# The second layer's norm of a two-layer transformer: its factors by Newton's steps on VectorE, spread to all partitions through DRAM and applied to x where it lies, instead of on token rows that are turned back

## The chip, the cores and the metric

The kernel runs on one core of a Trainium2 chip. The metric is the device time of one execution in microseconds, the median of several runs. A core has TensorE (PE in the profile, with its weight loads as PEld), VectorE (DVE), ScalarE (ACT), GpSimd (POOL) and SyncE (SP), which here only issues DMA transfers. The on-chip memory (SBUF) has 128 partitions; TensorE writes its results to a second, small memory, PSUM, in banks of 128 x 512 numbers. The first number of a shape is always the partitions.

## What is computed

Two layers on x of 2 batches x 2048 tokens x 256 features, all in float32. Each layer normalizes x over the features, runs attention and a gated side branch on the result, and adds their product to x. The first layer has full attention and a recurrent mixture of experts, the second has attention in a window of 64 tokens to either side and a mixture of eight low-rank experts.

```python
def _layernorm(x, axis=-1, eps=1e-05):
    m = jnp.mean(x, axis=axis, keepdims=True)
    v = jnp.var(x, axis=axis, keepdims=True)
    return (x - m) / jnp.sqrt(v + eps)
...
    x = L0_attn_x
    xn = _layernorm(x, axis=-1)
    s = _L0_attn_ref(xn, ...)
    g = _silu(_L0_ffn_ref(xn, ...))
    x = x + s * g
    xn = _layernorm(x, axis=-1)
    s = _L1_attn_ref(xn, ...)
    g = _silu(_L1_ffn_ref(xn, ...))
    x = x + s * g
    return x
```

The change concerns the second `_layernorm` only.

## The kernel before

**Layout.** x, its normalized form xn and the gates gt lie in SBUF for the whole kernel, one tile per batch, with features on partitions: [128, 2, 2048], the 256 features being two halves of 128. A block is 512 tokens; a batch has four. The mean and the variance of a token run over features, that is over partitions[...]. So the norm goes through token rows.

**The second norm before.** `norm_there` (L114 to L126) takes half a block, 256 tokens: TensorE turns x by four transposes of 128 x 128 into a PSUM bank with tokens on partitions, one copy (L120) puts that into xn, where it rests, and VectorE takes `bn_stats` (L123) and `bn_aggr` (L125), which give mean and variance per token. `factors` (L98 to L102) makes from them, for all 16 tiles of a batch or for eight at once, 1/sqrt(var + eps) by a ScalarE square root (L100) and a VectorE reciprocal (L101), and -mean times that (L102). A factor is then one number per partition, so `norm_apply` scales a row tile with one instruction (L131 on ScalarE, L133 on VectorE). `norm_back` (L135 to L143) turns the block back on TensorE, eight transposes (L139) into two banks, and copies them into xn (L143).

**Attention of the first layer.** It has 32 items (batch, group of four heads, block of 512 queries). An item takes 16 steps of 128 keys. In a step TensorE makes scores for a maximum of an item six steps ahead (`sq`, L671), scores of this item (`sk`, L671), and the product of the last step's exponentials with v (`acc`, L747). `sk`, `acc` and everything small share one ring of four PSUM banks. ScalarE takes the exponential; the products are summed up in `av`: by a ScalarE copy and a GpSimd add (L760, L761) as a rule, but in the last 22 steps by one VectorE add (L755) that reads the bank. An item that is complete is divided by its denominators through small DMA transfers on SP (`ad`, `dn`, `rd`, then `recb`, the reciprocals spread over the heads' partitions), the last of them a GpSimd multiply (`divide`, L801). The very last item takes a shorter way by TensorE transposes (`last_there` L809 to L813, `last_back` L825). `project` (L833) is the output projection; its result times the gate (`upd`, L838, VectorE, one buffer) is added to x by GpSimd (L840).

**The order of the work.** The program is written step by step, and `at(s, f)` hangs a function behind step s. Within an engine the instructions run in the order in which they are written, which a scheduler may shift where `pin` does not hold them. In the last 22 steps, which no longer have `sq` work, batch 0's `norm_there` calls hang two steps apart, eight of them. After the last step a written list does the rest of batch 0: apply, back, the last item's projection, and the router's `gates` (L966, copy L970) and `tokens` (L974, copy L976) of the second layer for every block, then `normalized` (a softmax over eight experts).

**The stage between the layers.** Batch 1 is normalized here. Its calls alternate by hand with the second layer's key and query projections of batch 0 (`keys_queries`, L469, 16 jobs, twelve of them placed among the norm's calls), which give TensorE work while the other engines do theirs. Transposes use a ring of two banks (tag `l`), projections one of four (tag `o`), gates and tokens one more. Then come the experts (L1021 to L1037) and the second attention, which the change does not touch.

Of the kernel before, what the change touches and what calls it, by code (L numbers as in the profile page):

```python
# [10 lines left out]
F32 = mybir.dt.float32  # L11
I32 = mybir.dt.int32
AF = mybir.ActivationFunctionType
ALU = mybir.AluOpType
# [3 lines left out]
P = 128  # L18
D = 256
NC = D // P  # L20
H = 16
HD = D // H
NG = 4
HP = 32
HV = HD + 1
DEN = HD - 1
TB = 512
# [11 lines left out]
def two_layers(ctx: ExitStack, tc: tile.TileContext, a, out):  # L39
# [58 lines left out]
    def factors(f, mv, issue=lambda i: i):  # L98

        issue(nc.scalar.activation(f[:, 0, :], mv[:, :, 1], AF.Sqrt, bias=eps_t))  # L100
        nc.vector.reciprocal(f[:, 0, :], f[:, 0, :])  # L101
        nc.vector.scalar_tensor_tensor(f[:, 1, :], mv[:, :, 0], -1.0, f[:, 0, :], ALU.mult, ALU.mult)  # L102


    def resting(b, n, half):
        return xn[b][:, half, bass.ts(n, TB)].rearrange("p (t d) -> p t d", d=D)

    def norm_there(b, n, half, bank, tmp, mv, copy, issue=lambda i: i):

        H2 = QT // 2  # L110
        xt = bank().rearrange("p (t d) -> p t d", d=D)
        for t in range(H2):
            for c in range(NC):
                i = nc.tensor.transpose(  # L114
                    xt[:, t, bass.ts(c, P)], x[b][:, c, bass.ds(n * TB + (half * H2 + t) * P, P)], ident
                )
                if t + c == 0:
                    issue(i)
        rest = resting(b, n, half)
        copy(rest, xt)  # L120
        st = tmp.tile([P, H2, 6], F32, name="st2", tag="st2", bufs=1)
        for t in range(H2):
            nc.vector.bn_stats(st[:, t, :], rest[:, t, :])  # L123
        for t in range(H2):
            nc.vector.bn_aggr(mv[:, half * H2 + t, :], st[:, t, :])  # L125

    def norm_apply(b, n, f):
        for t in range(QT):
            rest = resting(b, n, t // 2)[:, t % 2, :]
            if t % 2:  # L130
                nc.scalar.activation(rest, rest, AF.Identity, scale=f[:, 0, t : t + 1], bias=f[:, 1, t : t + 1])  # L131
            else:
                nc.vector.tensor_scalar(rest, rest, f[:, 0, t : t + 1], f[:, 1, t : t + 1], ALU.mult, ALU.add)  # L133

    def norm_back(b, n, bank):  # L135
        xb = [bank() for _ in range(NC)]
        for c in range(NC):
            for t in range(QT):
                nc.tensor.transpose(  # L139
                    xb[c][:, bass.ts(t, P)], resting(b, n, t // 2)[:, t % 2, bass.ts(c, P)], ident  # L140
                )
        for c in range(NC):
            (nc.scalar.copy, nc.vector.tensor_copy)[c](xn[b][:, c, bass.ts(n, TB)], xb[c])  # L143

    def layer_norms(blocks, tmp, ps, between=lambda r: None):

# [329 lines left out]
    def attention(A, scale, local, final, start=None, projected=False):  # L476
# [19 lines left out]
        with ExitStack() as st:  # L496
# [357 lines left out]
            def at(s, f, *args):  # L854
                after.setdefault(s, []).append((f, args))
# [26 lines left out]
                at(0, start)  # L882
            if not local:
                single = lambda: pm.tile([P, TB], F32, name="xb", tag="m")
                mv = op.tile([P, NT, 2], F32, name="mv", tag="mv")
                nf = op.tile([P, 2, NT], F32, name="nf", tag="nf")
                tile_of = lambda n: slice(n * QT, (n + 1) * QT)
                logit = {}

                def back(n):  # L890
                    norm_back(0, n, single)
                    logit[n] = ep.tile([P, TB], F32, name="sl", tag="e")[:, :P]
# [6 lines left out]
                for f, *args in (  # L899
                    (last_there, last),  # L900
                    (norm_apply, 0, 0, nf[:, :, tile_of(0)]),
                    (last_back, last),
                    (back, 0),
                    (norm_apply, 0, 1, nf[:, :, tile_of(1)]),
                    (project, last, 0),
                    (back, 1),
                    (project, last, 1),
                    (norm_apply, 0, 2, nf[:, :, tile_of(2)]),
                    (lambda: gates(single()[:, :P], logit[0], 0, 0),),
                    (norm_apply, 0, 3, nf[:, :, tile_of(3)]),  # L910
                    (back, 2),
                    (lambda: tokens(single()[:, :P], logit[0], 0, 0),),
                    (lambda: gates(single()[:, :P], logit[1], 0, 1),),
                    (back, 3),
                    (lambda: tokens(single()[:, :P], logit[1], 0, 1),),
                    (lambda: gates(single()[:, :P], logit[2], 0, 2),),
                    (lambda: gates(single()[:, :P], logit[3], 0, 3),),
                    (lambda: tokens(single()[:, :P], logit[2], 0, 2),),
                    (lambda: tokens(single()[:, :P], logit[3], 0, 3),),
                    (normalized, op, 0),  # L920
                ):
                    at(total, f, *args)
            fetch(0)
# [71 lines left out]
    with tc.tile_pool(name="gw", bufs=1) as gw, tc.tile_pool(name="tb", bufs=2) as tb, tc.tile_pool(  # L995
# [49 lines left out]
        with tc.tile_pool(name="pl", bufs=1, space=PSUM) as pl:  # L1045
            bank = lambda: pl.tile([P, TB], F32, name="xb", tag="l", bufs=2)
            small = lambda: pl.tile([P, TB], F32, name="s", tag="s")[:, :P]
            mv = gw.tile([P, NT, 2], F32, name="mv1")
            nf = gw.tile([P, 2, NT], F32, name="nf1")
            tile_of = lambda n: slice(n * QT, (n + 1) * QT)  # L1050
            two = lambda r: slice(2 * r * QT, 2 * (r + 1) * QT)
            sl = {}

            def there(n):
                for half in range(2):
                    norm_there(1, n, half, bank, tb, mv[:, tile_of(n), :], nc.scalar.copy)
# [22 lines left out]
            norm_apply(1, 0, nf[:, :, tile_of(0)])  # L1079
            norm_apply(1, 1, nf[:, :, tile_of(1)])  # L1080
            there(2)
            project(1)
            there(3)
            factors(nf[:, :, two(1)], mv[:, two(1), :])
            project(1)
            norm_back(1, 0, bank)
            project(1)
            logits(0)
            norm_back(1, 1, bank)
            project(1)  # L1090
            tokens(small(), sl[0], 1, 0)
            logits(1)
            norm_apply(1, 2, nf[:, :, tile_of(2)])
            norm_apply(1, 3, nf[:, :, tile_of(3)])
            project(2)
            tokens(small(), sl[1], 1, 1)
            norm_back(1, 2, bank)
            project(1)
            logits(2)
            norm_back(1, 3, bank)  # L1100
# [12 lines left out]
            for n in range(NB):  # L1113
                experts(1, n)()
# [72 lines left out]
```

## Time and profile before

| | us |
|---|---|
| median of 3 runs | 2532.57 (2530.11 to 2535.89) |
| the profiled execution, its own time | 2535.19 |
| its span in the profile | 2533.5 |
| last steps of the first attention (last 22 of 512) | to 2108 |
| rest of batch 0's norm and its router | 2108 to 2124 |
| batch 1's norm beside projections | from 2124 |

| group | line | count | mean ns |
|---|---|---|---|
| exponentials, ScalarE 128 x 512 | L687 | 2048 | 602 |
| scores, TensorE 32 x 512 | L671 | 5632 | 533 |
| weighted values, TensorE 128 x 512 | L747 | 4096 | 605 |
| sum of products, GpSimd 128 x 512 | L761 | 459 | 1265 |

The mean granted TensorE clock is 0.999 of full speed. Engine names in the profile are those given above; a line such as "L747" is a line of the kernel as printed. In a group, "out<-in" names the tiles written and read. In a timeline the first number is the start in us from the span's begin, the second how long the instruction or the row of like instructions ran, and the bracket behind it how long the engine had been idle before and which instruction of another engine it was waiting for.

### The profile page before, as it was taken

What the parts mean: (1) busy time and instruction counts of PE and PEld (TensorE: products, weight loads), DVE (VectorE), ACT (ScalarE), POOL (GpSimd) and SP (SyncE); (2) the same over time, 40 slices, a digit from 0 to 9 for tenths busy, and PEclk for the clock granted to TensorE, in tenths of its full rate; (3) what the DMA queues carried; (4) which work ended last, traced back from release to release, by engine and by line L of the source; (5) the groups of instructions that cost most, each with busy time, mean ns of one, the idle gap of its engine ahead of it and who ended that gap; (6) DMA issues with size and microseconds to landing.
All of it is one profiled execution on the core that took longest, in us unless ns stands there. A gap on an engine that the chain in (4) does not pass through costs nothing.

```text
span 2533.5 us, 47883 instructions
## 1 busy us (share of the span) xinstructions
PE 2511.0 (99%) x18896; PEld 1058.6 (42%) x18896; DVE 1697.5 (67%) x2741; ACT 1628.0 (64%) x3204; POOL 878.0 (35%) x827
## 2 busy tenths in 40 slices
PE   8999999999999999999999999999999999999999
PEld 6444444444333333333333333333333334457766
DVE  4143333258888888888777788888888765238986
ACT  5400000126888888888888888888888886237755
POOL 0000000201444444444444444444444420016887
PEclk9999999999999999999999999999999999999999
DMA  4031111220000000000000000000000002121221
GB/s 159 3 84 51 52 51 39 88 79 14 6 10 23 8 8 23 8 8 23 8 8 23 6 8 25 6 10 24 6 10 6 6 10 68 43 100 60 87 98 63
DMA packets 59733, 89.67 MB, mean 35 GB/s; under 512 B 21064, under 2 KB 25544, under 8 KB 58228
## 3 DMA queue, kind: packets, MB, share of 16 engines
q1 hardware_dynamic: 57636, 85.31, 10.3%
q8 instruction: 148, 2.42, 0.4%
q10 hardware_dynamic: 1872, 1.31, 0.2%
q14 instruction: 77, 0.63, 0.1%
HBM read 55.99 MB, written 22.59 MB: 31 GB/s over the span
## 4 chain that ended last, share of the span: by engine, by line
PE 80%; DVE 0%; ACT 0%; DMA 0%; issue 0%; POOL 0%; ACTq 0%; DVEq 0%
PE sk L671 25%; PE acc L747 23%; PE sq L671 20%; PE pp L469 5%; PE pr L833 2%; PE pp L529 2%; PE po L1025 1%; PE pt L1021 1%; PE po L1033 1%; PE xb L114 0%; PE xb L139 0%; PE pmx L723 0%; PE of L825 0%; PE pw L1008 0%; DMA recb<-rd 0%
## 5 line engine op out<-in xcount | busy, mean ns | idle before, releaser
L683 DVE TENSOR_REDUCE part<-sq 128x2 f32<-128x1024 f32 x1024 | 1207.0, 1221 | 287.6 <-PE sq L671 287.4
L687 ACT ACTIVATE e<-sk 128x512 f32<-128x512 f32 x2048 | 1057.5, 602 | 215.8 <-PE sq L671 204.6
L671 PE MATMUL sk<-q,k 32*128 32x512 f32 (+2 forms) x5632 | 1135.1, 533 | 1.2 <-ACT xn L687 0.9
L671 PE MATMUL sq<-k,q 31*128 31x512 f32 (+2 forms) x5120 | 1129.1, 569 | 0.5 <-DVE part L683 0.5
L761 POOL TENSOR_TENSOR av<-av,more 128x512 f32<-128x512 f32 x459 | 580.7, 1265 | 931.9 <-ACT more L760 925.2
L671 PEld LDWEIGHTS sk<-q,k 32*128 32x128 f32 x5632 | 521.4, 184 | 603.2 <-ACT e L687 519.0
L747 PE MATMUL acc<-e,v 128*32 128x512 f32 x4096 | 546.7, 605 | 0.0
L671 PEld LDWEIGHTS sq<-k,q 31*128 31x128 f32 x5120 | 403.1, 183 | 22.9 <-DVE part L683 12.6
L760 ACT COPY more<-acc 128x512 f32<-128x512 f32 x459 | 269.1, 586 | 0.0
L747 PEld LDWEIGHTS acc<-e,v 128*32 128x32 f32 x4096 | 81.8, 108 | 388.1 <-ACT e L687 379.0
L453 ACT ACTIVATE gt<-po 128x512 f32<-128x512 f32 x16 | 8.8, 594 | 321.1 <-PE po L449 321.1
L678 DVE CUSTOM_DVE_ANT_0 seen<-sq,mask 128x256 f32<-128x256 f32 (+1 forms) x512 | 175.7, 408 | 57.8 <-PE sq L671 54.3
L459 POOL TENSOR_TENSOR x<-x,up 128x512 f32<-128x512 f32 x16 | 25.1, 1589 | 450.1 <-DVE up L456 450.1
L440 DVE TENSOR_TENSOR xs<-we,px 128x512 f32<-128x512 f32 x64 | 44.0, 687 | 136.4 <-PE px L432 131.8
L692 POOL TENSOR_SCALAR_AFFINE_SELECT xn<-xn 128x512 f32<-128x512 f32 x172 | 106.2, 652 | 78.4 <-ACT xn L687 75.5
L432 PE MATMUL px<-xn,FV 128*128 128x512 f32 x256 | 121.2, 595 | 0.0
L436 PE MATMUL py<-cum,FW 128*128 128x512 f32 x256 | 120.5, 593 | 0.6 <-DVE cum L404 0.6
L416 PE MATMUL po<-pr,UO 128*128 128x512 f32 x256 | 119.0, 592 | 0.0
L687 ACT ACTIVATE xn<-sk 128x512 f32<-128x512 f32 x172 | 90.0, 600 | 41.6 <-PE sq L671 18.1
L442 DVE TENSOR_TENSOR pr<-xs,py 128x512 f32<-128x512 f32 x64 | 44.0, 688 | 64.4 <-PE py L436 64.2
L416 PEld LDWEIGHTS po<-pr,UO 128*128 128x128 f32 x256 | 48.6, 190 | 61.2 <-issue 61.2
L436 PEld LDWEIGHTS py<-cum,FW 128*128 128x128 f32 x256 | 48.4, 190 | 61.5 <-issue 59.8
(197 smaller groups left out, 1621.9 us busy)
## 6 DMA issues: line engine op xcount, KB each, us to landing
we<-wd SPq DMA_DIRECT2D x128, 128.0 KB
qd<-sb SPq DMA_DIRECT2D x48, 256.0 KB
xn<-av SPq DMA_DIRECT2D x59, 128.0 KB
recb<-rd SPq DMA_DIRECT2D x59, 128.0 KB
k<-qd SPq DMA_DIRECT2D x10, 512.0 KB
q<-qd SPq DMA_DIRECT2D x10, 512.0 KB
x<-in_x SPq DMA_DIRECT2D x8, 512.0 KB
qd<-elast SPq DMA_DIRECT2D x16, 256.0 KB
```

What stands on the lines that cost most here:

```text
L416: nc.tensor.matmul(po[oc], UO[:, ch, bass.ts(oc, P)], pr, start=(ch == 0), stop=False)
L432: nc.tensor.matmul(px, FV[:, c, bass.ts(ch, P)], xn[b][:, c, cols], start=(c == 0), stop=(c == NC - 1))
L436: nc.tensor.matmul(py, FW[:, c, bass.ts(ch, P)], cum[:, c, :], start=(c == 0), stop=(c == NC - 1))
L469: nc.tensor.matmul(ps, w[:, c, bass.ts(hf, P)], xn[b][:, c, bass.ts(n, TB)], start=(c == 0), stop=(c == NC - 1))
L671: nc.tensor.matmul(o, lhs, rhs, start=True, stop=True)
L678: nc.vector.tensor_tensor_reduce(seen[:, lo:hi], sq[:, d, t * 2 * P + lo : t * 2 * P + hi], mask[:, lo:hi], 1.0, LOWEST, ALU.add, ALU.max, ...
L683: nc.vector.tensor_reduce(pt[:, pair[0] : pair[1] + 1, t, kb], sq, AX.X, ALU.max)
L687: nc.scalar.activation(e, t, AF.Exp, scale=scale)
L692: nc.gpsimd.affine_select(out=e[:, :, c, :], in_=e[:, :, c, :], compare_op=ALU.is_ge, fill=0.0, base=0, pattern=[[0, 4], [sign, P]], chann ...
L747: nc.tensor.matmul(acc[hp[j], o : o + hi - lo], vs[b][:, kt, vcols(g, j)], es[j][:, lo:hi], start=(r == 0), stop=(r == len(parts) - 1), sk ...
L760: nc.scalar.copy(more, acc)
L761: nc.gpsimd.tensor_tensor(avs[i], avs[i], more, ALU.add)
```

## The change

- `norm_there` no longer copies the rows into xn; `bn_stats` reads the PSUM bank.
- `norm_factors`, new, makes the factors of one block (128 x 4 numbers, token rows on partitions) on VectorE alone: an integer first guess for 1/sqrt and four Newton steps of three instructions, then writes both factors into a tile `fac`, transposes it by 32 x 32 blocks, and SP writes the result (4 KB) to the DRAM tile `nd`.
- `norm_apply`, rewritten, reads the two rows of 512 factors back from `nd`, each spread over all 128 partitions (two DMA transfers on SP, 256 KB each), and multiplies and adds them onto x with features on partitions: four operations of 128 x 512 per block. For batch 0 all four are on GpSimd, in the two buffers of the tag `more`; for batch 1 one half of the features is on VectorE and the other on GpSimd, in four buffers of their own.
- `norm_back`, `resting` and the square root are gone from the second norm; the first layer's norm keeps `factors`.
- Batch 0: `norm_factors` follows the second half of each block, `norm_apply` two steps later, so three blocks are applied within the attention's steps. `logits` of blocks 0 to 2 hang behind the fourth, third and second last steps, those of block 3 and all tokens among `last_there` and `last_back`, `project` of the last item comes at the end.
- Batch 1: eleven projections are placed among the norm's calls in place of twelve, and in another order; five are left to the end instead of four.

```diff
     def norm_there(...)
-        rest = resting(b, n, half)
-        copy(rest, xt)
...
-            nc.vector.bn_stats(st[:, t, :], rest[:, t, :])
+            nc.vector.bn_stats(st[:, t, :], xt[:, t, :])
...
+    def norm_factors(b, n, tmp, mv):
+
+        s = tmp.tile([P, 3, QT], F32, name="root", tag="root", bufs=1)
+        v, y, w = s[:, 0, :], s[:, 1, :], s[:, 2, :]
+        nc.vector.tensor_scalar(v, mv[:, :, 1], EPS, None, ALU.add)
+        nc.vector.tensor_scalar(w.bitcast(I32), v.bitcast(I32), 1, None, ALU.logical_shift_right)
+        nc.vector.tensor_scalar(y.bitcast(I32), w.bitcast(I32), -1, 0x5F3759DF, ALU.mult, ALU.add)
+        for _ in range(4):
+            nc.vector.scalar_tensor_tensor(w, y, -0.5, v, ALU.mult, ALU.mult)
+            nc.vector.tensor_tensor(w, w, y, ALU.mult)
+            nc.vector.scalar_tensor_tensor(y, w, 1.5, y, ALU.add, ALU.mult)
+        nc.vector.tensor_copy(fac[:, 0, :, 0], y)
+        nc.vector.scalar_tensor_tensor(fac[:, 1, :, 0], mv[:, :, 0], -1.0, y, ALU.mult, ALU.mult)
+        turned = tmp.tile([P, HP], F32, name="tfac", tag="tfac", bufs=1)
+        nc.vector.transpose(turned, fac.rearrange("p k t e -> p (k t e)"))
+        nc.sync.dma_start(out=nd[b, n].rearrange("k t s r -> s (k t) r"), in_=turned[::4])
+
+    def norm_apply(b, n, place, engines):
+
+        m = [place() for _ in range(2)]
+        for k in range(2):
+            nc.sync.dma_start(
+                out=m[k], in_=nd[b, n, k].rearrange("t s r -> (t s r)").partition_broadcast(P)
+            )
+        cols = bass.ts(n, TB)
         for c in range(NC):
-            for t in range(QT):
-                nc.tensor.transpose(
-                    xb[c][:, bass.ts(t, P)], resting(b, n, t // 2)[:, t % 2, bass.ts(c, P)], ident
-                )
-        for c in range(NC):
-            (nc.scalar.copy, nc.vector.tensor_copy)[c](xn[b][:, c, bass.ts(n, TB)], xb[c])
+            engines[c].tensor_tensor(xn[b][:, c, cols], x[b][:, c, cols], m[0], ALU.mult)
+            engines[c].tensor_tensor(xn[b][:, c, cols], xn[b][:, c, cols], m[1], ALU.add)
...
                 for r in range(2 * NB):
                     n, half = divmod(r, 2)
-                    at(total - U - LEAD + 1 + 2 * r, norm_there, 0, n, half, single, op, mv[:, tile_of(n), :], nc.vector.tensor_copy, pin)
-                at(total - 1, factors, nf, mv, pin)
+                    s = total - U - LEAD + 1 + 2 * r
+                    at(s, norm_there, 0, n, half, single, op, mv[n], pin)
+                    if half:
+                        at(s, norm_factors, 0, n, op, mv[n])
+                        at(s + 2, norm_apply, 0, n, other, (nc.gpsimd, nc.gpsimd))
+
+                def logits(n):
+                    logit[n] = ep.tile([P, TB], F32, name="sl", tag="e")[:, :P]
+                    gates(single()[:, :P], logit[n], 0, n)
+
+                for n in range(NB - 1):
+                    at(total - NB + n, logits, n)
                 last = len(items) - 1
                 for f, *args in (
                     (last_there, last),
-                    (norm_apply, 0, 0, nf[:, :, tile_of(0)]),
+                    (logits, NB - 1),
+                    *((lambda n=n: tokens(single()[:, :P], logit[n], 0, n),) for n in range(NB - 1)),
                     (last_back, last),
-                    (back, 0),
...
+                    (lambda: tokens(single()[:, :P], logit[NB - 1], 0, NB - 1),),
+                    (normalized, op, 0),
+                    (project, last, 0),
+                    (project, last, 1),
...
             there(0)
-            project(2)
+            project(1)
             there(1)
-            factors(nf[:, :, two(0)], mv[:, two(0), :])
+            apply(0)
+            project(1)
+            there(2)
+            apply(1)
             whole_bias(A1, small())
+            project(1)
+            there(3)
+            apply(2)
+            project(1)
             turned(pl, 0)
             project(2)
...
+            apply(3)
             logits(0)
-            norm_back(1, 1, bank)
-            project(1)
+            project(2)
             tokens(small(), sl[0], 1, 0)
             logits(1)
...
             project(2)
             tokens(small(), sl[1], 1, 1)
...
             logits(2)
```

More of the change, by code (lines that the diff above doesn't have):

```diff
@@ L102, in factors, with norm_there @@
         nc.vector.scalar_tensor_tensor(f[:, 1, :], mv[:, :, 0], -1.0, f[:, 0, :], ALU.mult, ALU.mult)
-    def resting(b, n, half):
-        return xn[b][:, half, bass.ts(n, TB)].rearrange("p (t d) -> p t d", d=D)
-    def norm_there(b, n, half, bank, tmp, mv, copy, issue=lambda i: i):
+    nd = ctx.enter_context(tc.tile_pool(name="nd", bufs=1, space=bass.MemoryType.DRAM)).tile(
+        [B, NB, 2, QT, NG, HP], F32, name="nd"
+    )
+    fac = const.tile([P, 2, QT, 4], F32, name="fac")
+    nc.vector.memset(fac, 0.0)
+    def norm_there(b, n, half, bank, tmp, mv, issue=lambda i: i):
         H2 = QT // 2
@@ L118, in norm_there @@
                     issue(i)
-        rest = resting(b, n, half)
-        copy(rest, xt)
         st = tmp.tile([P, H2, 6], F32, name="st2", tag="st2", bufs=1)
         for t in range(H2):
-            nc.vector.bn_stats(st[:, t, :], rest[:, t, :])
+            nc.vector.bn_stats(st[:, t, :], xt[:, t, :])
         for t in range(H2):
             nc.vector.bn_aggr(mv[:, half * H2 + t, :], st[:, t, :])
-    def norm_apply(b, n, f):
-        for t in range(QT):
[L129 to L133, printed above, removed]
@@ L135, in norm_back @@
-    def norm_back(b, n, bank):
-        xb = [bank() for _ in range(NC)]
-        for c in range(NC):
-            for t in range(QT):
-                nc.tensor.transpose(
-                    xb[c][:, bass.ts(t, P)], resting(b, n, t // 2)[:, t % 2, bass.ts(c, P)], ident
-                )
-        for c in range(NC):
-            (nc.scalar.copy, nc.vector.tensor_copy)[c](xn[b][:, c, bass.ts(n, TB)], xb[c])
+    def norm_factors(b, n, tmp, mv):
[13 more added lines that the diff above has]
+        nc.sync.dma_start(out=nd[b, n].rearrange("k t s r -> s (k t) r"), in_=turned[::4])
@@ L145, in layer_norms @@
+    def norm_apply(b, n, place, engines):
[3 more added lines that the diff above has]
+                out=m[k], in_=nd[b, n, k].rearrange("t s r -> (t s r)").partition_broadcast(P)
+            )
+        cols = bass.ts(n, TB)
+        for c in range(NC):
+            engines[c].tensor_tensor(xn[b][:, c, cols], x[b][:, c, cols], m[0], ALU.mult)
+            engines[c].tensor_tensor(xn[b][:, c, cols], xn[b][:, c, cols], m[1], ALU.add)
     def layer_norms(blocks, tmp, ps, between=lambda r: None):
@@ L884, in attention @@
                 single = lambda: pm.tile([P, TB], F32, name="xb", tag="m")
-                mv = op.tile([P, NT, 2], F32, name="mv", tag="mv")
-                nf = op.tile([P, 2, NT], F32, name="nf", tag="nf")
-                tile_of = lambda n: slice(n * QT, (n + 1) * QT)
+                mv = [op.tile([P, QT, 2], F32, name=f"mv{n % 2}", tag=f"mv{n % 2}") for n in range(NB)]
+                other = lambda: op.tile([P, TB], F32, name="more", tag="more", bufs=2)
                 logit = {}
-                def back(n):
-                    norm_back(0, n, single)
-                    logit[n] = ep.tile([P, TB], F32, name="sl", tag="e")[:, :P]
                 for r in range(2 * NB):
                     n, half = divmod(r, 2)
-                    at(total - U - LEAD + 1 + 2 * r, norm_there, 0, n, half, single, op, mv[:, tile_of(n), :], nc.vector.tensor_copy, pin)
-                at(total - 1, factors, nf, mv, pin)
+                    s = total - U - LEAD + 1 + 2 * r
[8 more added lines that the diff above has]
+                    at(total - NB + n, logits, n)
                 last = len(items) - 1
@@ L900, in attention @@
                     (last_there, last),
-                    (norm_apply, 0, 0, nf[:, :, tile_of(0)]),
+                    (logits, NB - 1),
+                    *((lambda n=n: tokens(single()[:, :P], logit[n], 0, n),) for n in range(NB - 1)),
                     (last_back, last),
-                    (back, 0),
-                    (norm_apply, 0, 1, nf[:, :, tile_of(1)]),
+                    (lambda: tokens(single()[:, :P], logit[NB - 1], 0, NB - 1),),
+                    (normalized, op, 0),
                     (project, last, 0),
-                    (back, 1),
                     (project, last, 1),
[L908 to L920, printed above, removed]
                 ):
@@ L1047, in two_layers, with apply @@
             small = lambda: pl.tile([P, TB], F32, name="s", tag="s")[:, :P]
[L1048 to L1051, printed above, removed]
             sl = {}
             def there(n):
+                mv = tb.tile([P, QT, 2], F32, name="mv", tag="mv")
                 for half in range(2):
-                    norm_there(1, n, half, bank, tb, mv[:, tile_of(n), :], nc.scalar.copy)
+                    norm_there(1, n, half, bank, tb, mv)
+                norm_factors(1, n, tb, mv)
+            def apply(n):
+                norm_apply(1, n, lambda: tb.tile([P, TB], F32, name="fb", tag="fb", bufs=4), (nc.vector, nc.gpsimd))
             def logits(n):
@@ L1072, in two_layers @@
             there(0)
-            project(2)
+            project(1)
             there(1)
-            factors(nf[:, :, two(0)], mv[:, two(0), :])
+            apply(0)
+            project(1)
+            there(2)
+            apply(1)
             whole_bias(A1, small())
+            project(1)
+            there(3)
+            apply(2)
+            project(1)
             turned(pl, 0)
             project(2)
-            norm_apply(1, 0, nf[:, :, tile_of(0)])
-            norm_apply(1, 1, nf[:, :, tile_of(1)])
-            there(2)
-            project(1)
[L1083 to L1087, printed above, removed]
+            apply(3)
             logits(0)
-            norm_back(1, 1, bank)
-            project(1)
+            project(2)
             tokens(small(), sl[0], 1, 0)
             logits(1)
-            norm_apply(1, 2, nf[:, :, tile_of(2)])
-            norm_apply(1, 3, nf[:, :, tile_of(3)])
             project(2)
             tokens(small(), sl[1], 1, 1)
-            norm_back(1, 2, bank)
-            project(1)
             logits(2)
-            norm_back(1, 3, bank)
             project(1)
```

## The prediction

> **What bounds the kernel now.** I read the page's busy times first, then the chain of waits for the span and for the stretch around the change, then the timelines of TensorE, VectorE and GpSimd there.
>
> ```profile
> PE 2511.0 (99%) x18896; PEld 1058.6 (42%) x18896; DVE 1697.5 (67%) x2741; ACT 1628.0 (64%) x3204; POOL 878.0 (35%) x827
> PEclk9999999999999999999999999999999999999999
> PE 80%; DVE 0%; ACT 0%; DMA 0%; issue 0%; POOL 0%; ACTq 0%; DVEq 0%
> ```
>
> TensorE is busy in 99% of the span at full clock and carries the chain. So a microsecond of TensorE work removed is a microsecond gained, unless TensorE then waits. TensorE in the stretch itself (start, duration, line; in brackets the idle time before and its releaser):
>
> ```profile
> 2107.20 1.07 PE L747 MATMUL acc<-e,v 128*32 128x512 f32 x8
> 2109.62 0.66 PE L809 MATMUL tr<-ident,av 128*128 128x128 f32 x4 [1.36 <-DVE av L755]
> 2111.92 1.06 PE L825 MATMUL of<-ident,over 128*64 128x128 f32 x8 [1.64 <-DVE over L813]
> 2112.91 1.09 PE L139 MATMUL xb<-ident,xn 128*128 128x128 f32 x8
> 2113.84 1.88 PE L833 MATMUL pr<-xn,wo 128*128 128x512 f32 x4
> ...
> 2123.92 1.10 PE L114 MATMUL xb<-ident,x 128*128 128x128 f32 x8 [0.28 <-DVE lg L976]
> 2124.86 3.60 PE L469 MATMUL pp<-xn,wk 128*128 128x512 f32 x8
> ```
>
> Only 1.36 + 1.64 us of idle (and 0.28) stands here; until 2107 and from 2124 to 2222 TensorE is continuous. Every wait the change adds ahead of a TensorE instruction is therefore paid.
>
> **What is removed.** The eight groups of L139. From the start of a group to the next instruction: 0.93 + 0.87 + 0.93 + 0.92 for batch 0 and 0.88 + 0.93 + 0.87 + 0.93 for batch 1, in sum 7.26 us of TensorE. Logits and tokens of batch 0 are moved: 3 x 0.58 us into the last attention steps, the rest into the 1.36 and 1.64 us waits, which takes up to some 1.6 us more from the end. The copies (L120, L143), applies, the Sqrt and its table loads (1.28 us each on ScalarE) lie beside TensorE: gain nothing by themselves.
>
> **What is added on VectorE.** Per block 17 small operations on 128 x 4 and a 32 x 32 transpose, each needing the one before. The nearest pair:
>
> ```profile
> 2144.11 0.17 DVE L102 SCALAR_TENSOR_TENSOR nf<-mv,nf 128x8 f32<-128x8 f32 x1
> 2144.31 0.41 DVE L133 TENSOR_SCALAR xn<-xn,nf 128x256 f32<-128x256 f32 x1
> ```
>
> A dependent step is 0.20 us, an independent one about 0.09. So 16 x 0.20 + 0.09 + 0.21 (transpose) = 3.5 us per block. Now the tail, where VectorE frees TensorE's accumulator banks:
>
> ```profile
> 2085.30 0.69 DVE L755 TENSOR_TENSOR av<-av,acc 128x512 f32<-128x512 f32 x1 [1.41 <-PE acc L747]
> 2085.90 0.68 DVE L120 COPY xn<-xb 128x512 f32<-128x512 f32 x1
> 2086.62 0.75 DVE L123 BATCH_NORM_STATS2 st<-xn 128x6 f32<-128x256 f32 x2
> 2087.29 0.30 DVE L125 BATCH_NORM_AGGREGATE mv<-st 128x2 f32<-128x6 f32 x2
> 2088.03 0.69 DVE L755 TENSOR_TENSOR av<-av,acc 128x512 f32<-128x512 f32 x1 [0.44 <-PE acc L747]
> ```
>
> A pair of steps lasts 4.85 us, and VectorE has 1.41 + 0.44 of idle in it, plus 0.68 from the copy that goes: some 2.5 us. The 3.5 us lump stands ahead of the next `av` add, and behind that add TensorE waits for a bank of the ring of four. Stall: 0.35 us at the first block, where the ring is fresh, then 1.1, 1.0 and 1.0 once its slack is used: 3.45 us.
>
> **The lock.** Between the lumps GpSimd now applies the factors: four operations of 128 x 512 per block, 1.27 us each by L761 (1262 to 1275 ns), 5.1 us in a row. Newton's steps have two inputs in SBUF. What happens when such an operation meets a row of GpSimd operations, the two timelines show elsewhere, VectorE first:
>
> ```profile
> 2500.60 5.24 DVE L801 TENSOR_TENSOR xn<-xn,recb 64x512 f32<-64x512 f32 x1
> 2505.77 0.34 DVE L785 RECIPROCAL dn<-dn 64x32 f32<-64x32 f32 x1
> ```
>
> ```profile
> 2500.55 4.75 POOL L692 TENSOR_SCALAR_AFFINE_SELECT xn<-xn 128x512 f32<-128x512 f32 x8
> ```
>
> The same operation takes 0.69 us alone (fastest of its 14). Here it ended 0.54 us after the eight operations of GpSimd: it was shut out across all of them. Where three stand in a row it got in between (0.91). The Trainium skill, "SBUF — State Buffer", section "Who interferes with whom", says why: VectorE's second SBUF input shares GpSimd's read port under an exclusive lock, so the loser is blocked for the instruction. That rule speaks against this change: by it every Newton step is exposed; by the durations of small rows alone none is. No row here has a 4-column operation under GpSimd, so both ends stay: 0, and the whole burst.
>
> Whole burst: the factors go out with SP (write lands 1.8 us after issue, as `md` at 2049.57 lets its reader issue at 2051.36), the broadcast read of 256 KB lands 2.6 us after, so the burst runs from 4.5 to 9.6 us after a lump's end. The next lump starts 7.1 us after it (at 4.85 us a pair plus the stalls): shut out for 0.95, then 2.3 and 2.45 us. Stalls become 0.35, 2.1, 3.3 and 3.45 = 9.2 us instead of 3.45.
>
> That read is estimated so: `recb` (128 KB) took 3.64 us from issue to its reader with a quarter of the DMA engines busy. The Trainium skill, "DMA: Bandwidth & Descriptors", section "Why a DMA increments its semaphore by 16 and not by 1", has the number of engines divide the slowest dimension; `recb`'s is 4, the new read's 128, so all 16 would work. By the row 3.6 us, by the rule about 2.6 (`ge`, outermost 16, also 256 KB, lands in 2.7). I take 2.6; the row costs 1 more.
>
> **The queues of SP and GpSimd.** On SP each pair of reads waits for its factors' write to land and for GpSimd to leave the two buffers; `dn`, `rd` and `recb` of the last but one item queue behind such waits. That alone would cost little, as their reader on GpSimd now comes late anyway: L801 of that item, at 2086.78 before, is now behind all four bursts, and `pr` L833 needs it (2101.30 and 2105.28 before). Without lock: last factors 2097.7, landed 2099.6, read 2102.2, four applies and the divide of 1.27 each: 2108.6. TensorE would be there at 2106.85: 1.8 us of stall (2.8 by the `recb` row), 1.7 with the lock. Behind `pr` stand all of the last steps. From there to batch 1's first transposes 13.9 us, in it about 1.1 of waiting since `upd` has one buffer, which GpSimd's x update frees. Against 2123.92 before: 2123.45 without lock (-0.5), 2129.2 with it (+5.3).
>
> **Batch 1.** The same steps interleave with the statistics, on two banks, and behind VectorE's mask memset that waits for GpSimd (0.9). TensorE saves 3.6 us and waits in tokens(0) and gates(1), whose copies queue behind Newton and the VectorE half of an apply: about 1.1 + 1.25, net -0.4 to -1.3. With the lock (two GpSimd applies per block, 2.5 us in a row) the waits become 0.45 + 5.1 + 3.8 = 9.4: net +5.8. SP carries 24 more issues of about 0.55 us over 90 us: beside.
>
> **Clock.** A pause of 2.0 us in weight loads at 470 us brought a half clock for 3.4 us:
>
> ```profile
> 471.33 5.40 PE L469 MATMUL pp<-xn,wk 128*128 128x512 f32 x8 [1.17 <-ACT gt L453]
> ```
>
> 5.40 instead of 3.60: 1.8 us each time. The waits of 1.36 and 1.64 at 2108 did not do it. Without lock no stall is certain to; with it up to five are over 3 us.
>
> **The sum.** The profiled execution is 2535.19 us (span 2533.5), 2.6 above the median 2532.57; I add differences to the median. No lock: -0.5 - 0.9 = about -1. Whole lock: +5.3 + 5.8 = +11, and with one to three clock drops +13 to +16. A step that slips in between two GpSimd operations moves on, so I take a lock that bites for most, not all: +9, that is 2541.5.
>
> **Rivals.**
> 1. *Hides as meant* (faster): lumps pack tighter than 0.20 us, or the ring has more slack than I count, no lock: -7.3 and up to -1.6, less 1 to 2 that is left to wait: -6 to -8, 2525 to 2526. For: TensorE bound, VectorE at 67%. It needs a lump below 2.5 us, so a step below 0.14; the 0.20 row is against it.
> 2. *No lock on tiny operations* (same): -1, 2531.5. For: an operation of 0.15 us can win a gap between two of GpSimd's. Against: the row of eight. It decides if a lump in the tail takes 3.5 us under a burst.
> 3. *Late chain*: as forecast, but reads land at 3.6 us and `pr` waits more, clock drops added: +15, about 2547.
>
> **Chances.** Lock in part or whole 0.45; late chain with drops 0.17; no lock 0.25; as meant 0.13. 0.2% (5.1 us) is about the least that a measurement of this kernel can tell from no change. Faster is *as meant* but for its slowest edge (0.01): 0.12. Same is *no lock*, that edge and the weakest tenth of the forecast (0.04): 0.30. Slower is the rest of the forecast and the late chain: 0.58. The range takes in *no lock* below and the whole lock with two drops above: 2530 to 2550; it leaves out *as meant* and some 0.04 of the late chain. The forecast's own range is 2537 to 2547.
>
> **What would show it.** VectorE's Newton rows: 3.5 us per block alone, 5 to 6 where they overlap four GpSimd applies in a row. TensorE: new idle before `acc` and transposes in 2080 to 2110 released by VectorE, and before `pr` released by GpSimd; in batch 1 before tokens(0) and gates(1). L139 gone: 7.3 us. I am wrong if the small operations keep 0.20 us under GpSimd, if GpSimd's operations are the ones that wait, or if the ring's slack takes the lump.

## The result and the profile after

After the change the kernel takes 2547.55 us (median of 4 runs, 2545.44 to 2547.82) against 2531.34 us before (4 runs): a ratio of 1.0055, 95% interval 1.0043 to 1.0067. It is slower by 11 to 17 us. That lies in the range of the forecast (2530 to 2550) and on its side, but the loss is larger than the 9 us of the likeliest case.

The page of the profiled execution after the change (2547.7 us, span 2545.7): busy times, granted clock, and the chain by engine.

```profile
PE 2509.0 (99%) x18832; PEld 1051.3 (41%) x18832; DVE 1714.7 (67%) x2856; ACT 1606.3 (63%) x3165; POOL 911.3 (36%) x851
PEclk9999999999999999999999999999999999999999
PE 77%; DVE 2%; DMA 1%; POOL 1%; issue 0%; ACT 0%; SPq 0%; ACTq 0%; POOLq 0%; DVEq 0%
```

TensorE is busy 2 us less (64 transposes are gone), and VectorE, DMA and GpSimd have come onto the chain. What TensorE waits for between 2044 and 2240 us is in the view of the waits (who waited for whom: us in total, times, longest):

```profile
PE xb L119 <- DVE av L769: 4.3, 2, 2.3
PE s L979 <- DVE sl L975: 4.0, 1, 4.0
PE pr L847 <- POOL xn L815: 2.7, 1, 2.7
PE sk L685 <- DVE av L769: 2.0, 1, 2.0
PE xb L119 <- DVE upd L852: 1.3, 1, 1.3
PE tr L823 <- DVE av L769: 0.9, 1, 0.9
```

Lines have moved: L119 is `norm_there`'s transpose, L685, L761 the scores and `acc`, L769 the `av` add, L815 `divide`, L847 `project`, L852 its product with the gate, L971 to L981 gates and tokens. Three waits behind a Newton lump (2.0, 2.35 and 2.04 us), one before `pr`, one at batch 1's tokens(0). The first lump costs nothing.

**Where the time went, by stage.** The first layer, which no run here changes up to its last steps, gets through up to 5.8 us earlier or later from one execution to the next (one group of its first products took 1.99 us here and 3.78 before). So I measure the traces from marks inside: the start of VectorE's last transposition of the maxima (T, at 2049.33 before and 2046.54 after), the first transposes of batch 1 behind the last projection (X), and the second layer's value projections (Y).

| run | T to X, tail | X to Y, batch 1 | Y to end | sum |
|---|---|---|---|---|
| before | 74.59 | 98.37 | 311.21 | |
| after | +8.58 | +5.98 | +0.43 | +15.0 |

**The clock.** After some of these waits TensorE runs at half speed for a while. After the change, TensorE's timeline at the second block:

```profile
2071.77 1.18 PE L761 MATMUL acc<-e,v 128*32 128x512 f32 x8
2074.95 0.66 PE L119 MATMUL xb<-ident,x 128*128 128x128 f32 x4 [2.00 <-DVE av L769]
2075.54 1.33 PE L685 MATMUL sk<-q,k 32*128 32x512 f32 x8
2076.80 1.94 PE L761 MATMUL acc<-e,v 128*32 128x512 f32 x8
2078.67 1.66 PE L685 MATMUL sk<-q,k 32*128 32x512 f32 x8
2080.26 1.06 PE L761 MATMUL acc<-e,v 128*32 128x512 f32 x8
```

Eight `acc` take 1.94 us instead of 1.06, eight `sk` 1.66 instead of 1.14: 1.6 us lost behind a wait of 2.0. The granted clock in four stretches of the same trace (us from and to, length, busy time of PE, PEld, DVE, ACT and POOL with counts, then the clock, DMA share, GB/s):

```profile
2072.00:2082.00 10.00, 8.01 (x52) 2.23 (x50) 5.42 (x20) 5.63 (x12) 2.19 (x2) 0.83 0.23 68
2086.00:2096.00 10.00, 7.65 (x52) 2.34 (x48) 5.46 (x20) 5.28 (x11) 2.93 (x3) 0.83 0.24 68
2110.00:2120.00 10.00, 7.31 (x42) 2.34 (x46) 1.67 (x3) 2.24 (x5) 3.82 (x4) 0.83 0.09 28
2150.00:2165.00 15.00, 10.97 (x57) 4.52 (x50) 10.16 (x36) 0.99 (x2) 5.88 (x4) 0.77 0.44 134
```

By the rows that are too long the three drops in the tail cost 1.6 us each and the one in batch 1 2.6. By TensorE's busy time it is a little different: between T and X it is busy for 71.77 us, against 67.50 in e7 below, which has the same instructions there and no drop; between X and Y for 97.72 us, against 94.77 in e10. That makes 4.3 and 2.9, so about 7 us of the 15.

**The lock.** VectorE at the third block's lump, then GpSimd beside it:

```profile
2083.25 0.32 DVE L134 TENSOR_SCALAR root<-mv 128x4 f32<-128x4 f32 x1
2083.61 1.20 DVE L135 TENSOR_SCALAR root<-root 128x4 int32<-128x4 int32 x1
2084.84 0.17 DVE L136 TENSOR_SCALAR root<-root 128x4 int32<-128x4 int32 x1
2085.04 0.16 DVE L138 SCALAR_TENSOR_TENSOR root<-root 128x4 f32<-128x4 f32 x1
```

```profile
2082.28 2.49 POOL L157 TENSOR_TENSOR xn<-xn,more 128x512 f32<-128x512 f32 x2
```

An operation of 0.17 us takes 1.20 and ends when GpSimd's apply ends (2084.77). It is not one of those I had named: `tensor_scalar` has one input. After GpSimd is through, each step is back at 0.16. The second block's lump loses 1.03 us in the same way, but to GpSimd's x update (L854, 2069.83), which stands behind the first block's applies. In batch 1 it is the two-input steps that are shut out, in the same way (VectorE, then GpSimd):

```profile
2149.95 0.16 DVE L138 SCALAR_TENSOR_TENSOR root<-root 128x4 f32<-128x4 f32 x1
2150.14 1.12 DVE L139 TENSOR_TENSOR root<-root 128x4 f32<-128x4 f32 x1
2151.30 0.16 DVE L140 SCALAR_TENSOR_TENSOR root<-root 128x4 f32<-128x4 f32 x1
2151.49 1.12 DVE L138 SCALAR_TENSOR_TENSOR root<-root 128x4 f32<-128x4 f32 x1
```

```profile
2149.98 1.27 POOL L156 TENSOR_TENSOR xn<-x,fb 128x512 f32<-128x512 f32 x1 [1.48 <-DMA fb<-nd]
2151.33 1.26 POOL L157 TENSOR_TENSOR xn<-xn,fb 128x512 f32<-128x512 f32 x1
```

One VectorE operation gets in between two of GpSimd; the next waits for GpSimd's operation to end, and not for the whole row of them.

### The profile page after: what moved, and what is told of

It is laid out like the page before. It is cut to its first block, busy times and chain, and to the rows that moved or that the text cites. A ratio compares the mean times of both kernels' runs of the same rounds, so it can differ in the third digit from the quotient of the medians.

```text
span 2545.7 us, 47924 instructions
## 1 busy us (share of the span) xinstructions
PE 2509.0 (99%) x18832; PEld 1051.3 (41%) x18832; DVE 1714.7 (67%) x2856; ACT 1606.3 (63%) x3165; POOL 911.3 (36%) x851
## 4 chain that ended last, share of the span: by engine, by line
PE 77%; DVE 2%; DMA 1%; POOL 1%; issue 0%; ACT 0%; SPq 0%; ACTq 0%; POOLq 0%; DVEq 0%
PE sk L685 24%; PE acc L761 22%; PE sq L685 19%; PE pp L483 4%; PE pp L543 2%; PE pr L847 2%; PE po L1030 1%; PE po L1038 1%; PE pt L1026 0%; DMA fb<-nd 0%; DVE root L138 0%; PE pmx L737 0%; DMA recb<-rd 0%; PE of L839 0%; DVE root L139 0%
## 5 line engine op out<-in xcount | busy, mean ns | idle before, releaser
L685 PE MATMUL sk<-q,k 32*128 32x512 f32 (+2 forms) x5632 | 1137.6, 534 | 3.2 <-DVE av L769 2.0
L685 PE MATMUL sq<-k,q 31*128 31x512 f32 (+2 forms) x5120 | 1129.2, 569 | 0.5 <-DVE part L697 0.5
L685 PEld LDWEIGHTS sk<-q,k 32*128 32x128 f32 x5632 | 522.0, 185 | 605.3 <-ACT e L701 518.6
L761 PE MATMUL acc<-e,v 128*32 128x512 f32 x4096 | 548.3, 607 | 0.1
L685 PEld LDWEIGHTS sq<-k,q 31*128 31x128 f32 x5120 | 403.0, 183 | 22.8 <-DVE part L697 12.6
L761 PEld LDWEIGHTS acc<-e,v 128*32 128x32 f32 x4096 | 81.5, 108 | 390.0 <-ACT e L701 375.2
```

The costliest lines, as they stand in the source:

```text
L685: nc.tensor.matmul(o, lhs, rhs, start=True, stop=True)
L761: nc.tensor.matmul(acc[hp[j], o : o + hi - lo], vs[b][:, kt, vcols(g, j)], es[j][:, lo:hi], start=(r == 0), stop=(r == len(parts) - 1), sk ...
```

## The experiments

My theory: the tail's loss is lumps that exceed the ring's slack, lengthened by the lock, plus the place of the division in GpSimd's queue, and the half clock that such waits bring; batch 1's loss is the same lock. Rivals: the lump's own length, GpSimd's queue and late reads, or something at the seam of the two stages. The ratio of each run is to the kernel before on the same chip (2532.6 to 2532.7 us). Stage differences are from one trace each, against before. How far one trace can be trusted is seen where a run leaves a batch as the change has it. The tail is +8.58 after the change, and +7.1 to +7.7 in e1, e8 and e10, where bursts and lumps met at other moments: the wait behind the third block's lump is 3.35 to 3.88 us there, not 2.35. Batch 1 is +5.98 after the change, and +4.84 to +6.47 in e2 to e5 and e7. Differences smaller than these show nothing.

**e1 and e2: one batch at a time.** In e1 batch 1, in e2 batch 0 keeps the functions from before the change.

In e1, so for the stage between the layers:

```diff
             there(0)
-            project(1)
+            project(2)
             there(1)
-            apply(0)
-            project(1)
+            factors(nf[:, :, two(0)], mv[:, two(0), :])
...
```

> Only batch 0 has the new norm; batch 1 keeps square root, token rows and the way back. Theory (the two batches add up, each with its own waits on TensorE): the tail costs +8.6 us as the two traces show, batch 1 nothing: before +8 to +9, about 2540. Rival (the loss is made at the seam, by the late x update and the mask memset in front of batch 1's statistics): the seam is still there, so it would be near the whole change, +13 to +15.

> Only batch 1 has the new norm; the tail is as before. Theory: +6 us (4.0 us wait for tokens(0) behind VectorE's Newton steps, a clock drop after it, less 3.6 us of transposes), about 2537. Rival of the seam: batch 1 starts on time here, so no more than +1 to +2.

Measured: e1 2540.6 us, 1.0031 (1.0021 to 1.0042), tail +7.68, batch 1 0.00. e2 2541.42 us, 1.0028 (1.0016 to 1.0040), tail 0.00, batch 1 +4.84. Each batch alone loses in its own stage and nothing in the other. In the traces the two make 12.5 of the 14.6 us; by medians they make 7.9 + 8.7 us, a little more than the 14.9 of the whole (e2's traced execution, 2537.97 us, is one of its two short ones of six). So nothing large is made at the seam.

**e3: no applies on GpSimd in batch 0** (part of the computation is left out, see the expectation).

```diff
         for c in range(NC):
+            if b == 0:
+                continue
             engines[c].tensor_tensor(...)
```

> As the change, but GpSimd's four applies per block of batch 0 are left out (xn of batch 0 then holds the wrong numbers; the factors are made, written and read as before). Theory (half of the lump's excess is the lock, and pr waits for GpSimd's queue): no Newton row is longer than 0.2 us in the tail, stalls of about 1.0 us instead of 2.0 to 2.35, no wait before pr, no clock drop in the tail: 9 to 10 us less than the change, 2537 to 2538. Rival (the lump's own length makes the stalls, GpSimd only the wait at pr): stalls stay at 2 us with their clock drops, only 2.7 + 1.2 go: 2543 to 2544.

Measured: 2539.77 us, 1.0023 (1.0014 to 1.0032); tail +0.60. So 8.0 of the tail's 8.58 us come from GpSimd's applies and what follows from them; lumps by themselves make waits of 0.97 and 1.09 us without a clock drop. The third wait was 2.03 us with a drop, and my expectation of no long row was wrong by one: the division, which is still there, ran from 2089.01 for 1.28 us, and a Newton step that began at 2089.02 took 1.30. By medians e3 is 7.8 us below the change, short of the 9 to 10 expected.

**e4: the division early.**

```diff
-                    at(end + DEL + hop, f, i)
+                    at(end + DEL + hop - (2 if not local and f is divide and i == len(items) - 2 else 0), f, i)
```

> As the change, but the GpSimd division of the last but one item stands ahead of the fourth block's applies instead of behind them. Theory (pr waits 2.73 us for that place in the queue and the clock drops after it, 1.2): 3 to 4 us less than the change, about 2544. Rival (late reads of factors, the applies themselves needed next by the gates): the wait only moves to the gates of block 3 and tokens: 0 to 1 us less.

Measured: 2545.95 us, 1.0051 (1.0033 to 1.0069); tail +6.79. That is 1.8 less than after the change, and the medians differ by 1.6; the tail's own spread is about as large, so a gain is not shown, and the 3 to 4 us expected are not there. The wait before `pr` is gone, but the division now stands behind the third block's applies, and the last lump runs into it: two of its steps were shut out (1.20 and 1.13 us), the wait there grew from 2.04 to 3.03 us and brought a drop. The wait moved to the last lump; it did not go, and it did not move to the gates.

**e5: memsets in place of the applies** in batch 0, whose xn stays unnormalized.

```diff
         for c in range(NC):
+            if b == 0:
+                for k in range(2):
+                    for _ in range(3):
+                        nc.gpsimd.memset(m[k], 0.0)
+                continue
             engines[c].tensor_tensor(...)
```

The loop over `c` makes it twelve memsets per block, some 5.9 us in all, against 5.1 of the applies.

> As the change, but GpSimd's applies of batch 0 are replaced by three memsets each of the factor buffers, which only write and take about as long together (0.44 us each by the 128x4879 one); xn of batch 0 is left unnormalized, so its numbers are wrong. Theory (the lock is on reads: VectorE is shut out by a GpSimd operation that reads SBUF): no Newton row over 0.2 us in the tail, stalls as in the run without applies (1.0, 1.1, 2.0), only the wait before pr is back (about 2.2 us and a clock drop): the tail +4 against before instead of +8.6, in all about 2542. Rival (any GpSimd work beside VectorE slows it, or the queue of GpSimd alone is the cost): Newton rows of 1 us again, stalls of 2 us with their clock drops: as the change, 2547.

Measured: 2550.71 us, 1.0067 (1.0050 to 1.0084); tail +9.25, as bad as the change. That part of my theory, that only reads shut out, fell. The longest row is in the second block's lump: a `tensor_scalar` of 1.74 us, under GpSimd's x update, which reads, and the end of a memset before it; the wait behind that lump is 2.91 us. But the third block's rows say more. VectorE in e5:

```profile
2087.35 0.45 DVE L135 TENSOR_SCALAR root<-root 128x4 int32<-128x4 int32 x1
2087.84 0.45 DVE L136 TENSOR_SCALAR root<-root 128x4 int32<-128x4 int32 x1
2088.32 0.16 DVE L138 SCALAR_TENSOR_TENSOR root<-root 128x4 f32<-128x4 f32 x1
2088.52 0.16 DVE L139 TENSOR_TENSOR root<-root 128x4 f32<-128x4 f32 x1
```

And GpSimd over the same time, ten memsets of 0.49 us in a row until 2090.27:

```profile
2085.37 4.90 POOL L159 MEMSET more<- 128x512 f32 x10 [0.87 <-DMA more<-nd]
```

The one-input `tensor_scalar` waits for a memset to end; the two-input steps run on at 0.16 us under the next ones. So there are two ways to be shut out: a two-input operation by GpSimd's reads, a `tensor_scalar` by writes too. The second costs less here (0.8 and 0.6 us in the third and fourth lump); the tail is as long as after the change also because `pr` waits 3.37 us behind the longer burst, instead of 2.73. The Trainium skill, "SBUF — State Buffer", section "Who interferes with whom", has just this: `tensor_scalar` may run in a mode that takes both port pairs and then contends with GpSimd altogether, a two-input operation contends with reads only. I had used the second half and overlooked the first.

**e6: two Newton steps.**

```diff
-        for _ in range(4):
+        for _ in range(2):
```

> As the change, with two Newton steps instead of four: six small operations less per block, 1.2 us by the 0.20 us pitch. Theory (each stall is lump plus lock less the ring's slack, and a stall of 2 us brings the half clock): tail stalls of 0.8 to 1.3 us without clock drops; the wait for tokens(0) in batch 1 shorter by up to 2.4 us: 6 to 12 us less than the change, about 2538. Rival (GpSimd's bursts and the late reads set the pace, so a shorter lump meets more of the burst): 0 to 3 us less, 2545.

Measured: 2541.76 us, 1.0034 (1.0020 to 1.0047); tail +3.48, batch 1 +3.91: 7.6 us less in the traces, 5.8 by medians, at the lower end of the theory's 6 to 12. The second block's wait is gone, but the third block's lump, now earlier, met three of GpSimd's operations (1.20 + 1.20 + 1.18 us): a wait of 3.03 us with a drop. A shorter lump gains its difference in length, but how much of the burst the next one meets depends on where the two fall: e10, with four steps, loses 2.8 us in the same block.

**e7: the applies held until the next lump is over.** The full work, on the same engines; the reads (`norm_fetch`) keep their place, and the applies move behind the next block's factors. `last_turned` is the next block's `tfac`, so that the copy of one column holds GpSimd's queue until those factors are done. The division is early as in e4.

```diff
+        if b == 0 and n < NB - 1:
+            tc.keep_in_program_order(nc.gpsimd.tensor_copy(seen_turned, last_turned[0][:, :1]))
+        hold = tc.keep_in_program_order if b == 0 else lambda i: i
         for c in range(NC):
-            engines[c].tensor_tensor(...)
+            hold(engines[c].tensor_tensor(...))
...
-                        at(s + 2, norm_apply, 0, n, other, (nc.gpsimd, nc.gpsimd))
+                        if n:
+                            at(s, norm_apply, 0, n - 1, (nc.gpsimd, nc.gpsimd))
+                        at(s + 2, norm_fetch, 0, n, other)
...
```

> The whole computation. GpSimd starts the applies of a block of batch 0 only when the next block's factors are done (a tiny copy of those factors stands ahead of them on GpSimd), so that the applies fall between the lumps; the division of the last but one item stands ahead of the fourth block's applies. Theory (the lock, not the work, makes the second microsecond of each stall): no Newton row over 0.2 us in the tail, stalls of about 1.0, 1.1 and 2.0 us, no wait before pr: tail +0.6 to +1.5 against before as without applies, in all 2539 to 2540. Rival (the applies cost the tail in any place): tail +5 or more, 2544 and up.

Measured: 2537.44 us, 1.0016 (1.0009 to 1.0022), 10.1 us less than the change; tail -1.84, better than expected (the third wait, in e3 the one that met the division, is 0.95 here). TensorE's timeline of e7 at the three lumps:

```profile
2070.94 0.66 PE L119 MATMUL xb<-ident,x 128*128 128x128 f32 x4 [0.97 <-DVE av L782]
...
2081.84 0.66 PE L119 MATMUL xb<-ident,x 128*128 128x128 f32 x4 [1.15 <-DVE av L782]
...
2092.53 1.14 PE L698 MATMUL sk<-q,k 32*128 32x512 f32 x8 [0.95 <-DVE av L782]
```

The same lumps and the same applies, only not at the same time: the tail is 10.4 us shorter than after the change, 8.6 of them beyond what the early division gave in e4. No Newton row of the tail is longer than 0.17 us in its trace. This decides for the lock and against both the work and the lump's length; 0.97, 1.15 and 0.95 are what the lumps cost alone.

**e8: batch 1's copies on ScalarE,** in `gates` as shown, in `tokens` likewise.

```diff
-        nc.vector.tensor_copy(sl, pl)
+        (nc.scalar.copy if b else nc.vector.tensor_copy)(sl, pl)
```

> As the change, but batch 1's gates and tokens are copied out of PSUM by ScalarE instead of VectorE. Theory (TensorE waits 4.0 us at tokens(0) because the copy stands in VectorE's queue behind Newton steps shut out by the applies, then runs at half clock): that wait and the drop go, batch 1 at -1 to 0 against before instead of +6: 2540 to 2541. Rival (the wait is for the factors' late reads and moves to the next gates): less than 2 us gained, 2546.

Measured: 2549.03 us, 1.0058 (1.0043 to 1.0073); batch 1 +8.15. The wait of 4 us did not go: it moved to gates(1), which wait 4.06 us for the second block's xn, whose VectorE half stands behind the same blocked Newton steps. So the copy's place in the queue was not the cause, and the rival had the place right (the next gates). This run alone does not say whether late reads or the lock hold them.

**e10: batch 1 applied by VectorE alone.**

```diff
-                norm_apply(1, n, ..., (nc.vector, nc.gpsimd))
+                norm_apply(1, n, ..., (nc.vector, nc.vector))
```

> As the change, but batch 1 is applied by VectorE alone, so GpSimd is still there while VectorE does Newton's steps. Theory (of the wait of 4.0 us in batch 1 3.9 us are Newton steps and one apply shut out by GpSimd; VectorE gets four operations of 0.69 us more in their place before gates of block 1): no row over 0.2 us among the small ones, the wait 1 to 2.5 us shorter and its clock drop smaller or gone: 2 to 5 us less than the change, 2542 to 2545. Rival (VectorE's sheer work and the late reads make the wait, the lock doesn't): no less, 2547 or more.

Measured: 2544.32 us, 1.0036 (1.0022 to 1.0050); in the trace batch 1 is -0.14 instead of +5.98. The wait at tokens(0) is 1.66 us, and there is no drop after it:

```profile
2153.23 0.33 PE L979 MATMUL s<-ident,sl 128*128 128x128 f32 x1 [1.66 <-DVE sl L975]
```

Eight operations of 0.69 us more on VectorE, and 6 us less: between these two traces batch 1's loss is the lock and the drop behind it. The traced execution (2541.3 us) is the shortest of four; by medians e10 is only 3.2 us below the change, and no trace tells what the other three did. Late reads do not make the difference: the first block's still come 5.0 us after their issue (2139.74 to 2144.78), and VectorE idles 1.68 us for them as it idled 1.73 after the change. Whether they make the 1.66 us that are left, no run shows.

**e9 and e11: what the findings give.** e9 is e7 with two Newton steps in batch 0, batch 1 as before the change; e11 has e9's batch 0, and batch 1 new with VectorE alone and two steps.

> The whole computation. Batch 0 as in the run with the applies held between the lumps and the division early, with two Newton steps; batch 1 as before the change (square root, token rows, way back). Theory (with the lock avoided and a lump of 2.3 us within the ring's 2.5 us, nothing of the tail waits for the norm, and 3.65 us of transposes are saved): no stalls of 0.95 to 1.15 us any more, tail -1.84 - 3.07 = -4.9 against before, batch 1 at 0: 2527 to 2528. Rival (a shorter lump lets the applies or the divide collide again, or the end of the tail waits for the last apply): no better than -2, 2530 to 2531.

> The whole computation, both batches with the new norm: batch 0 as in e9 (held applies, early division, two Newton steps), batch 1 on VectorE alone with two Newton steps. Theory: tail -4.9, batch 1 shortened by the lock (3.9) and six steps less in each of the two lumps before tokens(0) (2.4), so between -2 and +2 instead of +6: 2526 to 2530. Rival (batch 1 is held by late reads of 3.4 to 5.1 us after issue, as the run with the copies on ScalarE showed the wait move to gates(1)): batch 1 at +3 or more, 2531 and up.

Measured: e9 2527.46 us, 0.9972 (0.9959 to 0.9984), tail -5.32, batch 1 -0.02: faster than both kernels. e11 2528.61 us, 0.9981 (0.9972 to 0.9989), tail -5.36, batch 1 +0.42. TensorE's waits in e9 in the same stretch:

```profile
PE xb L181 <- DVE upd L905: 1.3, 1, 1.3
PE tr L876 <- DVE av L822: 0.8, 1, 0.8
PE pp L596 <- ACT gt L1099: 0.7, 1, 0.7
PE pp L536 <- ACT v L600: 0.5, 1, 0.5
```

No wait for the norm is left in the tail: 3.65 us of transposes and 1.3 of the two old waits are gained, as the change could have done. In batch 1 e11 still waits 1.3 us for the last block's apply, whose reads queue on SP behind six other transfers, and 1.6 in four smaller waits; no run removes these. So e9 and e11 bear out the account of the tail. For batch 1 they show no gain: the new norm there is no faster than the old one.

## Why the prediction was right, and where it was not

- **What bounds, and that every wait is paid:** right. The tail's balance: 8.0 us more of waiting (11.4 in place of 3.4), 3.65 us of transposes less, 4.3 us of half clock: +8.6 worked out, +8.58 measured.
- **The lump:** 3.5 us forecast, 3.45 measured (2056.37 to 2059.82). Waits without the lock: 0.35, 1.1, 1.0, 1.0 forecast; 0, 0.97, 1.15, 0.95 in e7.
- **The lock:** right in kind, wrong in its terms. I had it shut VectorE out across the whole row of GpSimd's operations, by the row of 5.24 us; it does so until the running operation ends, and one of VectorE's gets in between, so 1.0 to 1.2 us are lost for each of GpSimd's operations met. The excess per block was 1.03, 1.18 and 1.08 us instead of 0.95, 2.3 and 2.45, and up to 3.1 where lump and burst met otherwise (e6); e10, with the same batch 0 as the change, had 1.1, 2.8 and none. And in the tail it hit the one-input steps.
- **GpSimd's queue before `pr`:** mechanism right, 2.73 us instead of 1.7 to 1.8. The reads were available to GpSimd 3.4 to 3.6 us after issue, not 2.6. The rule on the engines held (86% of the 16 busy in half a microsecond of the first reads, where `recb` had a quarter), but I had misread my row `ge`. In the trace before, the semaphores of the four `ge` reads from 2174 to 2180 us are counted up sixteen times each, for the first time 2.8 us after issue and for the last time after 3.65 to 3.9. I had taken the first for the landing, so that row too asked for the longer time.
- **The clock:** the failed term. "Without lock no stall is certain to; with it up to five are over 3 us" counted on drops for waits over 3 us only and left them out of the likeliest case. They came after waits of 2.00, 2.35, 2.73 and 4.03 us and cost about 7 us. Taken out of 15.0 this leaves about 8, against 9 forecast; that these lie so close is luck in part, as a lock too large per block stands against a wait before `pr` that was too small.
- **Batch 1:** +5.8 forecast with the lock, +5.98 measured, but by other terms, so the agreement is luck: waits of 5.9 us instead of 9.4, TensorE's work less by 2.9 us (by its busy time in e10) instead of 3.6, and 2.9 us of half clock that were not in the sum.
- **The rivals:** "hides as meant" needed a step below 0.14 us, which was 0.20. What it asks for can be had in another way: e9 hides all of it. "No lock" was refuted by the first trace; "late chain", with drops, at 2547, came nearest in size, and both of its terms, the later reads and the drops, were seen. (The sum of "no lock", -0.5 - 0.9, is -1.4 rather than "about -1"; nothing hangs on it.)

## What to carry to other kernels

Small VectorE operations in a dependent chain are not small beside GpSimd: each of GpSimd's operations that they meet can cost one full length of it, and `tensor_scalar` suffers even from memsets. Look where the two engines' bursts meet before moving work to GpSimd; if both must be there, order them in turn by a dependency, which here turned 6.8 us lost in the tail (e4) into 1.8 gained (e7) with the same work. And where TensorE is the bound, count a wait of 2 us and more nearly double, for the clock that it may bring down: here 1.6 us behind a wait of 2.00.

## What was not expected of the hardware

- Whether a wait brings the half clock down depends on where it falls. In each trace the half clock begins whole multiples of 3.41 us apart (after the change at 2076.36, 2090.01, 2113.91 and 2154.87, which is 4, 7 and 12 times 3.41). Cut the time from 2040 to 2240 us of all thirteen traces by each trace's own grid: each of the 24 stretches at full clock in which TensorE was idle for 1.89 us or more was followed by half clock, and none of the 694 with 1.74 us or less was. So the wait of 2.00 us, which fell into one stretch, had its drop, and the one of 2.04, which fell across two, had none. After the change (stretch, length, busy time of TensorE, then the clock, DMA share, GB/s):

```profile
2072.95:2076.36 3.41, 1.42 (x13) 1.00 0.02 3
2076.36:2079.77 3.41, 3.41 (x20) 0.50 0.63 191
2096.84:2100.25 3.41, 2.88 (x24) 1.00 0.02 5
2100.25:2103.67 3.42, 1.90 (x16) 1.00 0.01 1
```

Short waits add up: 1.37 and 0.61 us in one stretch of e8 brought a drop too. Once at half clock, 0.44 us of idle or more kept it there for a second stretch, as after the wait of 4.03 us. Idle time of the matmuls is not the whole condition: at 470 us a stretch with 1.17 us of it was followed by half clock in seven traces and in e7 not; in the other five the same wait fell across two stretches, and none followed. The Trainium skill, "TensorE: Matmul & The Clock Gate", Part 1, has the gate judge free-running windows of some 3.4 us, and the grid agrees; it names an idle window as what brings the half clock, where here 1.9 us of idle in one were enough.
- A VectorE operation that reads PSUM and one SBUF operand (the `av` add) keeps its 0.69 us under GpSimd's applies, and the `bn_stats`, which read PSUM, are not longer there either: only some forms meet the lock. And GpSimd can be the one that loses: in batch 1 its apply at 2145.39, begun just after one of VectorE's, took 1.77 us instead of 1.27.
